# Moving the second sample's soma products and gelu, and one GpSimd addition, in the start of a four-layer conditioned residual kernel

## The chip, the core and the metric

The kernel runs on one core of a Trainium2 chip. A core has a matrix engine (TensorE, PE in the profile; its weight loads are PEld), a vector engine (VectorE, DVE), an activation engine (ScalarE, ACT), GpSimd (POOL) and a queue that issues transfers (SyncE, SP). Each works off its own queue in order and waits on semaphores for the others. The metric is the device time of one execution in microseconds, the median of several runs.

## What is computed

The input x has 16 samples of 256 positions and 256 channels. Four layers follow one another, each added to its input:

```python
# layer 0, per sample: 16 causal traces
ctx      = causal_ema(x, tau_ctx)                      # h = alpha*h + b_t along the positions
gated    = x * sigmoid([x, ctx] @ Wg.T + bg)
mod      = 0.5 + sigmoid(gelu(x @ Wn1.T + bn1) @ Wn2.T + bn2)         # one row per trace
temporal = sum_d causal_ema(gated * mod[..., d], tau[d]) * softmax(blend)[d]
gate     = sigmoid(temporal @ Wtemp.T + btemp)
soma     = gelu(x @ Wsoma.T + bsoma)
x        = x + layernorm((soma * gate) @ Wout.T) * gamma + beta
# layer 1: pooling over the positions
scores   = tanh(x @ W1 + b1) @ v
x        = x + (softmax(masked scores) @ x) / count
# layer 2: 8 experts and a shared one, gated per sample
x        = x + sum_e coef[e] * ((silu(x @ Wg[e]) * (x @ Wu[e])) @ Wd[e])
# layer 3: gelu(x @ W1 + b1) @ [W2, We[index]] + bias, added to x
```

## The kernel before

**Precision.** A float32 operand is split into a rounded high part and the difference to it. A product is then three products on TensorE: high by high, high by low, low by high (`mm3`, L105 to L107). High parts are made by ScalarE's copy (`rnd`, L92), low parts by a subtraction on VectorE or GpSimd (`low`, L99). The small weights (gate, soma, temp, out and others) lie in `small_a` and `small_b` and are split into `wh` and `wl` by `high_small` (L141) and `low_small` (L99).

**Stages.** `traces(b)` is layer 0 of sample b up to the temporal sum, `pooled(b)` is the rest of layer 0 and layer 1. Layers 2 and 3 take the samples in pairs and stream expert weights in chunks (`w_e`) of 128 rows: `load_chunk` transfers a raw chunk (L792) into one of four raw places, ScalarE rounds it (L92), VectorE or GpSimd makes its low part (L99), and ten such chunks make a ring. A unit of layer 2 (`l2_unit`) makes `pg` and `pu` for two chunks, ScalarE's silu (L865), VectorE's product (L866), a split of the hidden layer (`hh`), and two units later the product back down (`y`). `pg` and `pu` share three PSUM buffers.

**The start.** Sample 0 goes first and alone through `first_traces` and `first_pooled`, which multiply unsplit float32. In `first_traces` ScalarE scales the modulation (L625), GpSimd multiplies it with the gated input (L628, traces 1 to 15), VectorE scans (L631) and TensorE sums the traces (L635). At its end GpSimd adds beta to sample 0's input `xt` (L655); the layer norm adds the result (L695). `first_pooled` is a chain: `pt` (L668), tanh, `po` (L682), statistics of the layer norm, a power on GpSimd (L690), L695, transposes `ptr` (L703), `pa` (L710), tanh (L714), the scores `psc` (L717), masked maximum (L725) and exp (L728), normalisation (L736), transposes `ppt` (L741), `pp` (L749), the sum `acc` (L753) and its split, with which layer 2 starts.

**Between these steps** stand those of the second sample, `second_traces` (L334): its context scan, `ph` and a gelu (L350), the gate products in two halves (`gates_of`, L363 to L365), the modulation, the soma products in two halves of six (`soma_half`), and two gelus into `sm` (L402). Then `blended` does its 16 traces: VectorE's products `bt` (L417) and scans (L421), GpSimd's running sum `ta` (L425), with modulation rows that SP loads in pairs (`mod`, L412).

**What sets the order.** `ORDER0` says by hand which of the two generators steps next (p: `first_pooled`, t: `second_traces`; each `yield` ends a step). `extra` puts other work behind numbered steps, `tc.issue_after(i)` puts instructions behind another in order of issue, and the framework's scheduler settles the rest for each engine. After the start, steps of the following samples are spread over the units of layer 2 by a pace (`pace`, `due`). Sample 0 goes alone through the first five experts; then sample 1 joins.

Of the kernel before, what the change touches and what calls it, by code (L numbers as in the profile page):

```python
# [8 lines left out]
F32 = mybir.dt.float32  # L9
F32R = mybir.dt.float32r  # L10
I32 = mybir.dt.int32
AF = mybir.ActivationFunctionType
ALU = mybir.AluOpType
# [4 lines left out]
S = 256  # L18
P = 128
# [3 lines left out]
RING = 10  # L23
FRONT = 4

ORDER0 = "pptptptptptptptptpt"
FRONT0 = ORDER0.count("t")
SECOND_STEPS = FRONT0 + 17
SLACK = 16
# [13 lines left out]
O_N1, O_G, O_SO, O_TE, O_OU, O_W1, W_COLS = 0, 256, 1280, 1792, 2304, 2816, 3072  # L43

V_BG, V_BN1, V_BN2, V_BSO, V_BTE, V_B1, V_V, V_L3B1, V_B2, V_WN2, V_COLS = 0, 2, 3, 4, 6, 8, 9, 10, 18, 19, 67
# [3 lines left out]
def fused_kernel(  # L49
# [21 lines left out]
    V, G, A, PE = nc.vector, nc.gpsimd, nc.scalar, nc.tensor  # L71
# [12 lines left out]
    ps_y = ctx.enter_context(tc.tile_pool(name="ps_y", bufs=1, space=PSUM))  # L84
# [3 lines left out]
    last_of = {}  # L88
# [9 lines left out]
    def low(e, out_, in_, h):  # L98
        i = (V if e == "v" else G).tensor_tensor(out_, in_, h.bitcast(F32), ALU.subtract)  # L99
        if e == "v":  # L100
            last_of["cv"] = i
        return i

    def mm3(o, wh, wl, xh, xl, start, stop, **kw):
        PE.matmul(o, wh, xh, start=start, stop=False, **kw)  # L105
        PE.matmul(o, wh, xl, start=False, stop=False, **kw)  # L106
        last_of["pe"] = PE.matmul(o, wl, xh, start=False, stop=stop, **kw)  # L107
# [7 lines left out]
    def load_xt(b):  # L115
        xt = xin.tile([P, 2, S], F32, tag="xt", name=f"xt{b}", bufs=1)
        nc.sync.dma_start(xt, x[b])
        return xt

    def const(shape, dtype, name, src, q=nc.scalar):  # L120
        t = cp.tile(shape, dtype, name=name)
        q.dma_start(t, src)
        return t
# [7 lines left out]
    def small(off, n):  # L131
        if O_TE <= off < O_W1:
            return raw_b[:, off - O_TE : off - O_TE + n]
        c = off if off < O_TE else off - O_W1 + O_TE
        return raw_a[:, c : c + n]
# [7 lines left out]
    def low_small(c0, n, e):  # L143
        low(e, wl[:, c0 : c0 + n], small(c0, n), wh[:, c0 : c0 + n])
# [6 lines left out]
    vec = const([P, V_COLS], F32, "vec", vecs)  # L151
# [7 lines left out]
    xt_tiles = {0: load_xt(0)}  # L159
    gam = const([P, S], F32, "gam", gamma.partition_broadcast(P), nc.sync)  # L160
    bet = const([P, S], F32, "bet", beta.partition_broadcast(P), nc.sync)
# [81 lines left out]
    def W(part, off, n):  # L243
        t = wh if part == 0 else wl
        return t[:, off : off + n]
# [13 lines left out]
    def ft(tag, name, bufs=1):  # L259
        return l0.tile([P, 2, S], F32, tag=tag, name=name, bufs=bufs)  # L260
# [68 lines left out]
    def soma_half(pso, xh, xl, m):  # L329
        for k in range(2):  # L330
            o = O_SO + k * S + m * P
            mm3(pso[:, m], W(0, o, P), W(1, o, P), xh[:, k], xl[:, k], k == 0, k == 1)

    def second_traces():  # L334


        xh, xl = early_x.pop(1)
        xr = xin_tiles.pop(1)
        cx = ft("ta", "ctx1")
        for c in range(2):  # L340
            V.tensor_tensor_scan(
                cx[:, c], decay[:, ND : ND + 1].to_broadcast([P, S]), xr[:, c], 0.0, ALU.mult, ALU.add
            )
        yield
        ph = ps_y.tile([P, 512], F32, tag="y1", name="ph1")
        for k in range(2):
            o = O_N1 + k * P
            mm3(ph[:, :S], W(0, o, P), W(1, o, P), xh[:, k], xl[:, k], k == 0, k == 1)
        hg = l0.tile([P, S], F32, tag="hg", name="hg1")
        last_of["ca"] = A.activation(hg, ph[:, :S], AF.Gelu, bias=vec[:, V_BN1 : V_BN1 + 1])  # L350
        ch, cl = hl("c_1", "hA")
        rnd("a", ch, cx)
        hs = l0.tile([P, S], F32R, tag="hs", name="hs1")
        rnd("a", hs, hg)
        pg = ps_y.tile([P, 2, S], F32, tag="y0", name="pg1")

        def gates_of(ks):
            for m in range(2):
                for k in ks:
                    o = O_G + k * S + m * P  # L360
                    i, j = (xh[:, k], xl[:, k]) if k < 2 else (ch[:, k - 2], cl[:, k - 2])
                    kw = dict(skip_group_check=True)
                    PE.matmul(pg[:, m], W(0, o, P), i, start=k == 0 and m == 0, stop=False, **kw)  # L363
                    PE.matmul(pg[:, m], W(0, o, P), j, start=False, stop=False, **kw)
                    last_of["pe"] = PE.matmul(pg[:, m], W(1, o, P), i, start=False, stop=k == 3, **kw)  # L365

        with tc.issue_after(last_of["chain"].ins):
            gates_of((0, 1))
        yield
        low("v", cl, cx, ch)  # L370
        yield
        low("v", hs[64:], hg[64:], hs[64:])
        yield
        pm = ps_gu.tile([P, 512], F32, tag="gu", name="pm1")
        with tc.issue_after(last_of["chain"].ins):
            PE.matmul(pm[:48, :S], n2[:, 0], hs, start=True, stop=False)
            last_of["pe"] = PE.matmul(pm[:48, :S], n2[:, 1], hs, start=False, stop=True)
        yield
        with tc.issue_after(last_of["chain"].ins):
            gates_of((2, 3))  # L380
        pso = ps_y.tile([P, 2, S], F32, tag="y1", name="pso1")
        with tc.issue_after(last_of["pe"].ins):
            soma_half(pso, xh, xl, 0)
        md = l0.tile([48, S], F32, tag="md", name="md1")
        A.activation(md, pm[:48, :S], AF.Tanh, bias=hb[:48, V_BN2 : V_BN2 + 1], scale=0.5)
        ga = ps_a.tile([P, 2, S], F32, tag="ga", name="gp1")
        for m in range(2):
            last_of["ca"] = A.activation(
                ga[:, m], pg[:, m], AF.Tanh, bias=hb[:, V_BG + m : V_BG + m + 1], scale=0.5
            )  # L390
        yield
        V.tensor_scalar(md, md, 0.5, 1.0, ALU.mult, ALU.add)
        mdd = dram.tile([1, ND, S], F32, tag="mdd", name="mdd1")
        nc.sync.dma_start(mdd[0], md[0:ND])
        yield
        last_of["cv"] = V.scalar_tensor_tensor(ga, ga, 1.0, xr, ALU.add, ALU.mult)
        yield
        with tc.issue_after(last_of["chain"].ins):
            soma_half(pso, xh, xl, 1)
        sm = ft("sm", "sm1")  # L400
        for m in range(2):
            last_of["ca"] = A.activation(sm[:, m], pso[:, m], AF.Gelu, bias=vec[:, V_BSO + m : V_BSO + m + 1])  # L402
        yield
        yield from blended(1, ga, mdd, sm, None)

# [159 lines left out]
    def first_traces():  # L565
# [27 lines left out]
        ms = l0.tile([48, S], F32R, tag="ths", name="ms0")  # L593
        rnd("v", ms, md)
        low("v", ms[32:], md[32:], ms[32:])

        with tc.issue_after(last_of["md"].ins):
            for off in (O_G, O_G + 512):
                high_small(off, 512)
        for off in (O_G, O_G + 512):  # L600
            low_small(off, 512, "g")
        yield
        ga = ft("ga", "ga0")
        with tc.issue_after(last_of["pm"].ins):
# [8 lines left out]
        sm = ps_a.tile([P, 2, S], F32, tag="ga", name="sm0")  # L613

        tacc = [ps_y.tile([P, 512], F32, tag=f"y{c}", name=f"ta0{c}")[:, :S] for c in range(2)]
        for d in range(ND):
# [19 lines left out]
            if d == 5:  # L636
                pso = ps_l.tile([P, 2, S], F32, tag="ps", name="pso0")
# [5 lines left out]
            if d in (9, 11):  # L643
                m = (d - 9) // 2
# [5 lines left out]
        for c in range(2):  # L650
            evict(c, t[:, c], tacc[c])
        last_of["t"] = last_of["ca"]
        xt = xt_tiles.pop(0)
        with tc.issue_after(last_of["g"].ins):
            last_of["g"] = G.tensor_tensor(xt, xt, bet.unsqueeze(1).to_broadcast([P, 2, S]), ALU.add)  # L655
        held[0] = xt, sm, t
        yield

# [340 lines left out]
    def prefetch(n, boost=BOOST, later=None):  # L999
        while n > 0 and nxt[0] < len(order):  # L1000
            k = order[nxt[0]]
            if k[0] == "c" and k[1] not in eregs:
                eregs[k[1]] = nc.sync.value_load(eix[0:1, k[1] : k[1] + 1], min_val=0, max_val=NE - 1)
            with tc.high_priority(offset=boost) if boost else nullcontext():
                load_chunk(k, later)
            nxt[0] += 1
            n -= 1
# [24 lines left out]
    def feed():  # L1032
        gens, left = {}, {}
        for i, phase in enumerate(phases):
# [14 lines left out]
            live = set(phase)  # L1049
            fixed = list(ORDER0) if i == 1 else []  # L1050
            while live:
# [38 lines left out]
        high_small(O_SO, 512)  # L1090
        low_small(O_SO, 512, "g")

    low_later = []

    def high_parts():
        prefetch(2, 0, low_later)
        for off, n in ((O_TE, 512), (O_OU, 512), (O_W1, 256)):
            high_small(off, n)

    def low_parts(*small_ones):  # L1100
        while low_later:
            low(*low_later.pop(0))
        for off, n in small_ones:
            low_small(off, n, "v")

# [1 line left out]
        5: high_parts,  # L1107
        9: low_parts,
        15: lambda: low_parts((O_TE, 512)),
        17: lambda: low_parts((O_OU, 512), (O_W1, 256)),  # L1110
    }
    with tc.issue_after(last_of["t"].ins):
        weights_on_gpsimd()
    for i in range(1, len(ORDER0) + 1):
        beside(lambda: next(steps))
        if i in extra:
            beside(extra[i])
    n = 4
    with tc.issue_after(last_of["ca"].ins), tc.issue_after(last_of["cv"].ins):
        coefs()  # L1120
        prefetch(RING - n)
# [155 lines left out]
```

## Time and profile before

| What | us |
|---|---|
| three runs | 2819.82, 2822.01, 2822.59 (median 2822.01) |
| the profiled execution | 2821.16 |
| its span, from the first to the last instruction | 2819.1 |
| TensorE busy / VectorE / ScalarE / GpSimd | 2769.4 / 1455.0 / 1242.8 / 1301.6 |
| mean granted TensorE clock | 0.996 of full |
| TensorE busy, 300 to 2819 | 2505.6 of 2519.0 |
| TensorE busy, 160 to 180 | 10.4 of 20, granted clock 0.74 |
| VectorE busy, 70 to 120 | 50.0 of 50 |
| GpSimd busy, 70 to 120 | 46.5 of 50 |

A row of a timeline is: start, duration, engine, line, operation, output and inputs, shapes, and in brackets the idle time of the engine before it with what ended it. In order of time the start looks so: first traces to 35.3, layer norm about 42, scores about 48, layer 2 from 55.5, silu from 62.2. From 164 to 174 TensorE is mostly idle; it then has no more work of sample 0 alone, and `pooled(1)` is not through yet. Full-clock products of 128x256 follow one another every 0.12 us there, and every 0.21 us at half clock. The names `gp` and `sm` are the second sample's gate and soma, `pso` the PSUM of its soma products.

### The profile page before, as it was taken

What the parts mean: (1) busy time and instruction counts of PE and PEld (TensorE: products, weight loads), DVE (VectorE), ACT (ScalarE), POOL (GpSimd) and SP (SyncE); (2) the same over time, 40 slices, a digit from 0 to 9 for tenths busy, and PEclk for the clock granted to TensorE, in tenths of its full rate; (3) what the DMA queues carried; (4) which work ended last, traced back from release to release, by engine and by line L of the source; (5) the groups of instructions that cost most, each with busy time, mean ns of one, the idle gap of its engine ahead of it and who ended that gap; (6) DMA issues with size and microseconds to landing.
All of it is one profiled execution on the core that took longest, in us unless ns stands there. A gap on an engine that the chain in (4) does not pass through costs nothing.

```text
span 2819.1 us, 37035 instructions
## 1 busy us (share of the span) xinstructions
PE 2769.4 (98%) x13636; PEld 2337.7 (83%) x13636; DVE 1455.0 (52%) x2664; ACT 1242.8 (44%) x2060; POOL 1301.6 (46%) x984
## 2 busy tenths in 40 slices
PE   8889999999999999999999999999999999999999
PEld 6878798888888888888888888888888888888888
DVE  7989876766665453544545445454444542222222
ACT  6555564565444433435334443334433453333334
POOL 5946545644554453544534444443444443333333
PEclk9999999999999999999999999999999999999999
DMA  5543376395443533324433143331523252222453
GB/s 144 164 137 107 103 251 215 117 321 189 152 158 106 174 109 109 116 81 152 142 113 99 48 174 110 116 119 53 177 101 113 92 170 91 90 90 90 168 177 118
DMA packets 116998, 377.53 MB, mean 134 GB/s; under 512 B 12898, under 2 KB 31186, under 8 KB 116818
## 3 DMA queue, kind: packets, MB, share of 16 engines
q1 hardware_dynamic: 116386, 375.11, 40.5%
q8 instruction: 108, 1.77, 0.3%
q14 instruction: 72, 0.59, 0.1%
q10 hardware_dynamic: 432, 0.06, 0.0%
HBM read 310.91 MB, written 64.21 MB: 133 GB/s over the span
## 4 chain that ended last, share of the span: by engine, by line
PE 88%; DVE 6%; ACT 2%; issue 2%; DMA 2%; SPq 0%; DVEq 0%; POOL 0%; ACTq 0%
PE pg L105 9%; PE pg L106 9%; PE pg L107 9%; PE pu L105 8%; PE pu L107 8%; PE pu L106 8%; PE y L107 8%; PE y L105 8%; PE y L106 8%; DVE w_e L99 1%; DVE tr L421 1%; PE z L105 1%; PE z L106 1%; PE z L107 1%; DMA raw_e<-in_wexp_dram 1%
## 5 line engine op out<-in xcount | busy, mean ns | idle before, releaser
L99 POOL TENSOR_TENSOR hh<-h,hh 128x512 fp32r<-128x512 f32 x640 | 848.2, 1326 | 1314.2 <-ACT hh L92 1294.8
L866 DVE TENSOR_TENSOR h<-h,pu 128x512 f32<-128x512 f32 x576 | 393.7, 683 | 904.4 <-PE pu L107 809.0
L92 ACT ACTIVATE hh<-h 128x512 fp32r<-128x512 f32 x640 | 403.6, 631 | 954.8 <-DVE h L866 932.1
L105 PE MATMUL pg<-x,w_e 128*128 128x512 f32 (+1 forms) x1232 | 465.8, 378 | 8.9 <-DVE h L866 8.9
L865 ACT ACTIVATE h<-pg 128x512 f32<-128x512 f32 x576 | 342.5, 595 | 298.0 <-PE pg L107 235.1
L105 PE MATMUL pu<-x,w_e 128*128 128x512 f32 (+1 forms) x1232 | 464.7, 377 | 7.0 <-ACT h L865 6.0
L106 PE MATMUL pg<-x,w_e 128*128 128x512 f32 (+1 forms) x1232 | 463.9, 377 | 0.0
L107 PE MATMUL pg<-x,w_e 128*128 128x512 f32 (+1 forms) x1232 | 463.6, 376 | 0.0
L106 PE MATMUL pu<-x,w_e 128*128 128x512 f32 (+1 forms) x1232 | 463.5, 376 | 0.0
L107 PE MATMUL pu<-x,w_e 128*128 128x512 f32 (+1 forms) x1232 | 463.4, 376 | 0.0
L106 PE MATMUL y<-hh,w_e 128*128 128x512 f32 (+1 forms) x1232 | 462.6, 376 | 0.6 <-POOL hh L99 0.6
L107 PE MATMUL y<-hh,w_e 128*128 128x512 f32 (+1 forms) x1232 | 462.4, 376 | 0.0
L105 PE MATMUL y<-hh,w_e 128*128 128x512 f32 (+1 forms) x1232 | 415.6, 376 | 0.0
L425 POOL TENSOR_TENSOR ta<-ta,tr 128x512 f32<-128x512 f32 x225 | 311.1, 1382 | 66.2 <-DVE tr L421 55.2
L421 DVE TENSOR_TENSOR_SCAN tr<-decay,bt 128x256 f32<-128x256 f32 x450 | 284.6, 671 | 0.0
L105 PEld LDWEIGHTS pg<-x,w_e 128*128 128x128 f32 x1232 | 232.3, 189 | 51.8 <-DVE h L866 11.8
L105 PEld LDWEIGHTS pu<-x,w_e 128*128 128x128 f32 x1232 | 232.6, 189 | 49.7 <-ACT h L865 7.8
L106 PEld LDWEIGHTS y<-hh,w_e 128*128 128x128 f32 x1232 | 231.9, 188 | 43.3 <-POOL hh L99 1.8
L107 PEld LDWEIGHTS pu<-x,w_e 128*128 128x128 f32 x1232 | 232.5, 189 | 41.9
L107 PEld LDWEIGHTS pg<-x,w_e 128*128 128x128 f32 x1232 | 232.0, 188 | 41.8
L107 PEld LDWEIGHTS y<-hh,w_e 128*128 128x128 f32 x1232 | 231.8, 188 | 41.9
L106 PEld LDWEIGHTS pu<-x,w_e 128*128 128x128 f32 x1232 | 232.4, 189 | 40.8
(308 smaller groups left out, 3275.0 us busy)
## 6 DMA issues: line engine op xcount, KB each, us to landing
w_e<-keep_e SPq DMA_DIRECT2D x216, 768.0 KB, 4.3
keep_e<-w_e SPq DMA_DIRECT2D x72, 768.0 KB, 4.3
raw_e<-in_wexp_dram SPq DMA_DIRECT2D x112, 384.0 KB, 4.5
mod<-mdd SPq DMA_DIRECT2D x120, 256.0 KB, 3.8
w_f<-keep_f SPq DMA_DIRECT2D x56, 384.0 KB, 3.5
spare<-in_wexp_dram SPq DMA_DIRECT2D x48, 384.0 KB, 3.2
raw_c<-in_comb_dram SPq DMA_DIRECT2D x32, 260.0 KB, 2.9
xr<-in_xT_dram SPq DMA_DIRECT2D x16, 256.0 KB, 3.3
```

The source lines that it names most:

```text
L92: last_of["ca"] = A.activation(out_, in_, AF.Copy)
L99: i = (V if e == "v" else G).tensor_tensor(out_, in_, h.bitcast(F32), ALU.subtract)
L105: PE.matmul(o, wh, xh, start=start, stop=False, **kw)
L106: PE.matmul(o, wh, xl, start=False, stop=False, **kw)
L107: last_of["pe"] = PE.matmul(o, wl, xh, start=False, stop=stop, **kw)
L421: V.tensor_tensor_scan(tr[:, c], decay[:, d : d + 1].to_broadcast([P, S]), bt[:, c], 0.0, ALU.mult, ALU.add)
L425: G.tensor_tensor(tacc, tacc, tr, ALU.add)
L865: A.activation(h, ps_g, AF.Silu)
L866: last_of["h"] = V.tensor_tensor(h, h, ps_u, ALU.mult)
```

## The change

Four edits, all in the first 65 us of the program.

1. **Soma products.** All twelve products of the second sample's soma are issued behind the first half of its gate products, ahead of the transposes `ptr`. Before, six stood behind the second half of the gate products, ahead of `ppt`, and six behind `pp`.
2. **Gelu.** The two gelus into `sm` stand ahead of the scores: behind the eviction of `ptr`, ahead of tanh at L714. In the built program ScalarE has one table load fewer. `second_traces` has one step fewer, and `ORDER0` one t fewer.
3. **Beta.** GpSimd's addition of beta to sample 0's `xt` moves from the end of `first_traces` to its second step. The two weight differences of the gate (`low_small`, GpSimd) are issued behind it.
4. **Chunk 4.** One chunk more is loaded in the start: its rounding on ScalarE stands ahead of the split of sample 0's `x`, its low part on VectorE behind that split.

Each engine runs as many products, traces and differences as before. The scheduler also orders many instructions between about 60 and 155 us differently: on VectorE products `bt` stand further ahead of scans, on GpSimd some `hh` and `w_e` differences change places with running sums, and on SP some `mod` loads stand ahead of chunk loads. Behind that the order is the same.

```diff
-ORDER0 = "pptptptptptptptptpt"
+ORDER0 = "pptptptptptptptptp"
...
         with tc.issue_after(last_of["chain"].ins):
             gates_of((0, 1))
+        pso = ps_y.tile([P, 2, S], F32, tag="y1", name="pso1")
+        with tc.issue_after(last_of["pe"].ins):
+            for m in range(2):
+                soma_half(pso, xh, xl, m)
         yield
         low("v", cl, cx, ch)
         yield
         low("v", hs[64:], hg[64:], hs[64:])
+        sm = ft("sm", "sm1")
+        for m in range(2):
+            last_of["ca"] = A.activation(sm[:, m], pso[:, m], AF.Gelu, bias=vec[:, V_BSO + m : V_BSO + m + 1])
         yield
...
         with tc.issue_after(last_of["chain"].ins):
             gates_of((2, 3))
-        pso = ps_y.tile([P, 2, S], F32, tag="y1", name="pso1")
-        with tc.issue_after(last_of["pe"].ins):
-            soma_half(pso, xh, xl, 0)
...
         last_of["cv"] = V.scalar_tensor_tensor(ga, ga, 1.0, xr, ALU.add, ALU.mult)
-        yield
-        with tc.issue_after(last_of["chain"].ins):
-            soma_half(pso, xh, xl, 1)
-        sm = ft("sm", "sm1")
-        for m in range(2):
-            last_of["ca"] = A.activation(sm[:, m], pso[:, m], AF.Gelu, bias=vec[:, V_BSO + m : V_BSO + m + 1])
         yield
...
         low("v", ms[32:], md[32:], ms[32:])
+        xt = xt_tiles.pop(0)
+        last_of["xt"] = G.tensor_tensor(xt, xt, bet.unsqueeze(1).to_broadcast([P, 2, S]), ALU.add)
...
-        for off in (O_G, O_G + 512):
-            low_small(off, 512, "g")
+        with tc.issue_after(last_of["xt"].ins):
+            for off in (O_G, O_G + 512):
+                low_small(off, 512, "g")
...
-        xt = xt_tiles.pop(0)
-        with tc.issue_after(last_of["g"].ins):
-            last_of["g"] = G.tensor_tensor(xt, xt, bet.unsqueeze(1).to_broadcast([P, 2, S]), ALU.add)
         held[0] = xt, sm, t
...
-    low_later = []
+    low_later, low_last = [], []
...
-    def low_parts(*small_ones):
-        while low_later:
-            low(*low_later.pop(0))
+    def low_parts(*small_ones, of=low_later):
+        while of:
+            low(*of.pop(0))
...
         15: lambda: low_parts((O_TE, 512)),
+        16: lambda: prefetch(1, 0, low_last),
         17: lambda: low_parts((O_OU, 512), (O_W1, 256)),
+        18: lambda: low_parts(of=low_last),
...
-    n = 4
+    n = 5
     with tc.issue_after(last_of["ca"].ins), tc.issue_after(last_of["cv"].ins):
         coefs()
         prefetch(RING - n)
```

## The prediction

> **What bounds the kernel now.** I read the page's busy rows first, then windows of TensorE as long as a step of its granted clock, then the timeline of each engine over the first 65 us, then the chain from there to 200.
>
> ```profile
> span 2819.1 us, 37035 instructions
> PE 2769.4 (98%) x13636; PEld 2337.7 (83%) x13636; DVE 1455.0 (52%) x2664; ACT 1242.8 (44%) x2060; POOL 1301.6 (46%) x984
> ```
>
> TensorE is the bound, and the change adds and removes none of its products. A change can act only on the 50 us in which TensorE idles and on the time it runs at half clock. Both lie mostly before 200: after 300 TensorE is busy 2505.6 of 2519.0. All edits lie before 65, and from about chunk 42 the order of every queue is the old one. So the question is what moves before 200.
>
> The window view (columns: window, length, PE busy and count, granted clock, DMA share, GB/s):
>
> ```profile
> 41.17:44.58 3.41, 1.56 (x12) 1.00 0.54 156
> 44.58:47.99 3.41, 3.27 (x8) 0.50 0.56 129
> 48.00:51.41 3.41, 3.41 (x15) 0.50 0.77 244
> 51.41:54.82 3.41, 2.99 (x19) 1.00 0.26 88
> 58.24:61.65 3.41, 1.89 (x16) 1.00 0.24 62
> ```
>
> The layer norm leaves TensorE busy for 1.56 of 3.41 us, and the next two windows run at half clock; a window with 1.89 did not lose it.
>
> The timeline of GpSimd, the tile view of beta, and the timeline of ScalarE:
>
> ```profile
> 11.78 2.68 POOL L99 TENSOR_TENSOR wl<-small_a,wh 128x512 fp32r<-128x512 f32 x2 [10.39 <-ACT wh L141]
> 15.56 18.44 POOL L628 TENSOR_TENSOR bt<-ga,mod 128x512 f32<-128x512 f32 x15 [1.11 <-ACT mod L625]
> 33.97 1.26 POOL L655 TENSOR_TENSOR xt<-xt,bet 128x512 f32<-128x512 f32 x1
> ```
>
> ```profile
> L122 SPq DMA_DIRECT2D bet<-in_beta_dram x1: 430/430/430, 7.7 to 7.7; - x1
> DMA to landing us min/median/max: 6.4/6.4/6.4
> ```
>
> ```profile
> 54.99 0.85 ACT L92 ACTIVATE x<-acc 128x256 fp32r<-128x256 f32 x2 [2.11 <-DVE acc L753]
> 55.86 1.28 ACT L402 ACT_TABLE_LOAD   x1
> 57.16 0.84 ACT L402 ACTIVATE sm<-pso,vec 128x256 f32<-128x256 f32 x2
> 57.88 0.84 ACT L92 ACTIVATE w_e<-raw_e 128x768 fp32r<-128x768 f32 x1
> 58.62 1.57 ACT L92 ACTIVATE w_e<-spare 128x768 fp32r<-128x768 f32 x2
> 60.09 0.84 ACT L92 ACTIVATE w_e<-raw_e 128x768 fp32r<-128x768 f32 x1
> 60.94 1.28 ACT L865 ACT_TABLE_LOAD   x1
> 62.24 1.09 ACT L865 ACTIVATE h<-pg 128x512 f32<-128x512 f32 x2
> ```
>
> GpSimd makes the fifteen trace products without a gap, and the last scan ends at 35.31, one pair (1.3) after the last product: GpSimd paces the first traces. In the last fence ScalarE goes from the split of the first sample to the first silu through a table load, a gelu, four chunk casts and a second load, while TensorE, with its three PSUM buffers full, waits 2.76 (its next product is at 62.89).
>
> **Part 1: beta.** GpSimd's addition now stands first in its queue and waits for beta. That landed at 7.75 + 6.4 = 14.15; the transfers ahead of it are unchanged. The addition ends at 14.15 + 1.26 = 15.4, the two weight differences queued behind it (2.68) at 18.1, and the first product on GpSimd starts there and not at 15.56: **+2.5**. Ends: 0 if beta landed before 10, +3.0 if the addition is stretched (1.74 is the longest at L433). I take 2.5, since it is the same transfer. ScalarE's scalings, the scans and TensorE's sums wait for these products, so the whole first chain moves. The 1.26 given back at 33.97 buys nothing on the chain: the power at L690 follows 0.1 behind the weight difference of the soma products, but waits for VectorE's L689, which is late by 2.5 too. That difference ends at 41.96 + 2.5 - 1.26 = 43.2, and the moved soma products first need it about 44.5.
>
> **Part 2: soma products in the gap.** Before, the gate products end issue at 41.78 and the transposes start at 43.43: a gap of 1.65. Twelve products at the pitch of 0.12 fill 1.44; cost nothing, with 0.2 to spare. What they may bring is the clock: 1.56 + 1.44 = 3.0 in that window, above the 1.89 that held full clock. At full clock pa (L710, four in 2.06) costs what two pairs at L668 do, 0.43 + 0.59 = 1.0, and psc (L717, 1.22) about 0.65. tanh and the exp table load come 1.0 earlier, the maxima 1.6; the first exp (48.88) waits for both, the load would end at 47.4: **-1.4**. The Trainium skill speaks against this (TensorE: Matmul & The Clock Gate, "HAM oscillation"): only idle gaps over about 3.4 us cost the clock. By it a gap of 1.65 did no harm, and filling it is worth 0; by the windows it is worth 1.4. The granted clock did fall here, so I take 1.4, with 0 as the other end.
>
> The six products removed at 51.03 stood between the normalised scores (ready 50.92) and their transposes (51.91): **-0.95**. The six at 54.58 ran while x was split (54.99): 0.
>
> First unit's products: 2.5 - 1.4 - 0.95 = +0.15, so 55.6 for 55.48.
>
> **Part 3: ScalarE.** The load and the gelu go: 57.88 - 55.86 = 2.02. The gelu, still within gelu's and tanh's table (no load stands between L350 and L714), goes behind the eviction ending 44.48 and ahead of tanh at 46.63; with the shorter pa 1.1 us remain for 0.84. If that cover were gone it would cost up to 0.84. Chunk 4's cast (pitch 0.74) moves into the idle 2.11 ahead of 54.99, its transfer issued at 38.95. ScalarE is thus ahead by 2.76 - 0.15 = **2.6**: silu at 59.6, just as TensorE fills its third buffer. The Trainium skill (ScalarE: Activation LUTs, "What ACT_TABLE_LOAD costs") prices a switch at 2.66, a drain of 1.38 included; by it this part gains 4.0. But here the load starts 0.02 behind x and the gelu 0.02 behind the load, so I take 1.28.
>
> VectorE's waits of 1.83, 1.24 and 0.66 before its first h (62.87) shrink alike: h at 60.2. From 62.87 to 121.4 VectorE has no idle gap in its timeline, so it carries these 2.6 us through the second sample's traces.
>
> **Part 4: order.** The scheduler reshuffles the queues from 60 to 155. On GpSimd one hidden-layer difference (1.3) comes ahead of the last running sum, on VectorE one h (0.66) ahead of t; VectorE starts t 2.0 after that sum, so only the 0.66 counts: **+0.6**. On SP the mod loads of traces 10, 12 and 14 step ahead of chunk loads 19, 20 and 23; each waits for a VectorE product that now comes earlier, and a late one holds the chunk behind it (3.3 to landing). Ends 0 and +3.3; I take 0. At 164 to 193 TensorE waits for the second sample, so its arrival sets the end: -2.6 + 0.6 = **-2.0**.
>
> The profiled execution took 2821.16 (span 2819.1), 0.85 below the median of 2822.01. So 2819.2 for it, and **2820.0** for the median.
>
> **Rivals.**
>
> *More comes than was moved (0.25).* The chain has soft places downstream. VectorE idles 0.98 and 1.47 between 121 and 125 for casts that waited on chunks, and TensorE runs 18 products from 173.9 at 0.21 and not 0.12 because the wait for the second sample cost its clock (1.7). Without them: -2.6 - 2.45 - 1.7 = -6.8, 2815.2. For it: fewer waits early give chunks a lead. Against: the same four raw buffers limit that lead.
>
> *A chunk wait gets ahead of the traces (0.23), slower.* ScalarE, VectorE and SP are queues in order. In the new order VectorE does two chunk differences (10, 11) between the fourth products and the third scans. A turn is transfer, cast and difference:
>
> ```profile
> 98.68 3.28 DMA raw_e<-in_wexp_dram
> 118.81 3.60 DMA spare<-in_wexp_dram
> 163.53 3.13 DMA spare<-in_wexp_dram
> ```
>
> Three such transfers are on the chain already. Each more costs 3.3 + 0.85 + 0.96 = 5.1; with two of them: -2.0 + 10.2 = +8.2, 2830.2. It decides from the second on. For it: VectorE has no slack there. Against: the transfers the new order needs first are issued some 2.6 earlier too.
>
> *The clock falls all the same (0.07).* Then 1.4 is lost and silu is ahead by about 1.2: -0.6, 2821.4. That the soma products do nothing for time is this case.
>
> **How the numbers follow.** The main case has 0.45, from -4.5 (order free, +0.6 gone, a half-clock window of 3.41 us less, 1.7) to +1 (beta's 3.0, gelu's 0.84, one window more); 0.05 of it spills past -5.6. A measurement of this kernel tells about 0.2% (5.6 us) from no change. Faster: 0.25 + 0.05 = 0.30; slower: 0.22 of the third case; same: 0.48. The range takes in the more-case down to 2813.5 and half of the slower case, to 2829.0; the main case alone is 2817.5 to 2823.
>
> **What would show it.** GpSimd's first trace product at 18.1, the layer norm's transposes near 45.9 with twelve soma products ahead; full clock in every window from 41 to 55; ppt near 52; no table load between ppt and the first silu; that silu near 59.6 and TensorE's wait before it below 0.5; VectorE without gaps from 60 on; the second sample's t at 124.5. If beta lands earlier, part 1 falls and the gain grows by up to 2.5; if the first trace product is late but VectorE shows new gaps on chunk casts between 65 and 120, the slower case is there.

## The result and the profile after

| | before | after |
|---|---|---|
| median of 11 runs | 2820.88 us | 2827.27 us |
| range | 2818.89 to 2825.07 | 2825.16 to 2831.49 |
| the profiled execution | 2821.16 | 2826.54 |

The ratio is 1.0023, with a 95% interval of 1.0015 to 1.0032: slower by 6.4 us, where 2820.0, 2.0 below the median known then, and no visible difference were forecast.

The first two lines of the page of the changed kernel:

```profile
span 2824.8 us, 37031 instructions
...
PE 2775.0 (98%) x13636; PEld 2343.3 (83%) x13636; DVE 1461.8 (52%) x2664; ACT 1240.5 (44%) x2059; POOL 1301.1 (46%) x984
```

VectorE does as many instructions as before in 6.8 us more: some of them take longer. Where the 5.7 us of span arise is seen by following the same instructions in both traces (starts in us; the last column is after less before):

| milestone | before | after | |
|---|---|---|---|
| first trace product on GpSimd | 15.56 | 18.49 | +2.9 |
| sample 0's t on ScalarE | 35.52 | 41.27 | +5.8 |
| split of sample 0's x | 54.99 | 58.02 | +3.0 |
| first silu | 62.24 | 62.33 | +0.1 |
| first h on VectorE | 62.87 | 64.81 | +1.9 |
| sample 1's t on ScalarE | 124.64 | 132.45 | +7.8 |
| split of sample 1's x | 184.12 | 190.47 | +6.3 |
| silu at 2745 | 2744.99 | 2750.63 | +5.6 |

Nearly everything is decided before 190; from there to the end the silus are 5.3 to 6.4 late. There are two losses, at 15 to 41 and at 60 to 130, and between them gains of the size that was forecast.

**The first loss.** The timeline of GpSimd, that of TensorE, and the window view in steps of 3.41 us (window, length, PE busy and count, then the other engines, granted clock, DMA share, GB/s), all of the changed kernel:

```profile
14.35 1.27 POOL L595 TENSOR_TENSOR xt<-xt,bet 128x512 f32<-128x512 f32 x1 [12.96 <-DMA bet<-in_beta_dram]
15.58 2.94 POOL L99 TENSOR_TENSOR wl<-small_a,wh 128x512 fp32r<-128x512 f32 x2
18.49 11.08 POOL L629 TENSOR_TENSOR bt<-ga,mod 128x512 f32<-128x512 f32 x9
```

```profile
20.52 1.80 PE L636 MATMUL ta<-tr,ident 128*128 128x256 f32 x4 [2.12 <-DVE tr L632]
22.25 0.79 PE L621 MATMUL pb<-ms,sel 48*128 48x256 f32 x2
22.97 3.78 PE L636 MATMUL ta<-tr,ident 128*128 128x256 f32 x8
```

```profile
17.20:20.61 3.41, 1.29 (x7) 0.77 (x5) 1.11 (x3) 0.84 (x2) 3.41 (x4) 1.00 0.99 390
20.61:24.02 3.41, 3.41 (x9) 2.07 (x10) 3.41 (x6) 2.24 (x7) 3.41 (x4) 0.53 0.14 51
...
30.85:34.26 3.41, 3.41 (x15) 2.36 (x15) 2.75 (x6) 1.06 (x3) 2.56 (x3) 0.97 0.00 0
```

GpSimd waits for beta and the traces start 2.9 late, as forecast within 0.4. But TensorE, which sums the traces, has too little to do meanwhile: it is busy for 1.29 of 3.41 us. The clock falls for 10.2 us, eight sums take 3.78 and not 1.99, VectorE's scans then wait for TensorE, and +2.9 becomes +5.8.

**The gains.** The layer norm's windows and ScalarE's timeline, changed kernel:

```profile
41.09:44.50 3.41, 3.41 (x18) 2.80 (x18) 1.10 (x3) 2.60 (x6) 3.41 (x3) 1.00 0.20 23
44.50:47.92 3.42, 3.42 (x24) 3.21 (x24) 3.30 (x10) 3.39 (x7) 1.78 (x3) 1.00 0.62 207
```

```profile
58.02 0.80 ACT L92 ACTIVATE x<-acc 128x256 fp32r<-128x256 f32 x2 [1.43 <-DVE acc L751]
...
61.04 1.28 ACT L863 ACT_TABLE_LOAD   x1
62.33 0.60 ACT L863 ACTIVATE h<-pg 128x512 f32<-128x512 f32 x1
```

The layer norm keeps full clock, and from t to the split of x 2.7 us are won against the profile of before (forecast 2.35). This is not shown to be the work of the moved soma products. Three of the kernels below (e2, e8, e16) leave the soma products where they were, and each has its window over the layer norm at another place than the profile of before. The window view of TensorE alone, of e8, e2 and e16 in this order:

```profile
40.01:43.42 3.41, 1.91 (x16) 1.00 0.57 202
43.42:46.84 3.42, 2.21 (x17) 1.00 0.39 121
39.16:42.58 3.42, 2.29 (x17) 1.00 0.66 229
```

They keep full clock there, and from t to the split of x they take 17.05, 16.74 and 17.03 us; the changed kernel takes 16.75, and only the profile of before takes 19.47. So the moved products win nothing where the clock holds; how often the kernel before loses it there is open.

One table load stands between the split and the silu: another 2.9 (2.76).

**The second loss.** VectorE's timeline before (first fence) and in the changed kernel, and the one line of GpSimd's beside the latter:

```profile
56.22 0.18 DVE L239 COPY coef<-sgt 128x16 f32<-128x16 f32 x1
56.43 0.17 DVE L240 TENSOR_SCALAR sgt<-sgt 128x16 f32<-128x16 f32 x1
```

```profile
59.19 0.95 DVE L99 TENSOR_TENSOR w_e<-raw_e,w_e 128x768 fp32r<-128x768 f32 x1
60.06 1.84 DVE L239 COPY coef<-sgt 128x16 f32<-128x16 f32 x1
61.93 1.76 DVE L240 TENSOR_SCALAR sgt<-sgt 128x16 f32<-128x16 f32 x1
63.73 0.29 DVE L241 TENSOR_TENSOR coef<-gat,sgt 128x128 f32<-128x128 f32 x1
63.94 0.95 DVE L99 TENSOR_TENSOR w_e<-raw_e,w_e 128x768 fp32r<-128x768 f32 x1
64.81 0.68 DVE L864 TENSOR_TENSOR h<-h,pu 128x512 f32<-128x512 f32 x1
```

```profile
59.63 4.03 POOL L99 TENSOR_TENSOR w_e<-spare,w_e 128x768 fp32r<-128x768 f32 x2 [6.08 <-ACT w_e L92]
```

Before, the copy and the scaling of the coefficients (16 columns) took 0.18 and 0.17. Chunk 4's low part (59.19) now stands ahead of them, so they come beside GpSimd's pair of differences. GpSimd's first difference ends at 61.86 and the copy at 61.90; the second ends at 63.66 and the scaling at 63.69: each waits for GpSimd's running instruction, 3.3 us in all, of which 1.9 reach h (the silu it needs ends at 62.9).

The pair of differences has moved too: it starts 1.6 behind the split of x and not 4.5, since ScalarE's casts come earlier there. This alone is enough. In e5, which has the moved gelu and no chunk 4, the pair starts 2.35 behind the split, and the next two instructions wait for it:

```profile
55.69 0.17 DVE L239 COPY coef<-sgt 128x16 f32<-128x16 f32 x1
...
56.96 1.94 DVE L241 TENSOR_TENSOR coef<-gat,sgt 128x128 f32<-128x128 f32 x1
58.83 2.58 DVE L99 TENSOR_TENSOR w_e<-raw_e,w_e 128x768 fp32r<-128x768 f32 x1
```

h comes 6.8 behind the split of x in e5 and e7, without chunk 4, as in the changed kernel with it.

From the first h to 134 it is VectorE's chunk differences that grow. The groups by form, before (56 to 130) and in the changed kernel (56 to 134):

```profile
L99 DVE TENSOR_TENSOR w_e<-raw_e,w_e 128x768 fp32r<-128x768 f32 x10 | 13.6, 1364 | 4.5 <-ACT w_e L92 4.5
L99 DVE TENSOR_TENSOR w_e<-spare,w_e 128x768 fp32r<-128x768 f32 x8 | 10.2, 1274 | 1.0 <-ACT w_e L92 1.0
...
L99 DVE TENSOR_TENSOR w_e<-raw_e,w_e 128x768 fp32r<-128x768 f32 x10 | 15.9, 1590 | 2.2 <-ACT w_e L92 2.2
L99 DVE TENSOR_TENSOR w_e<-spare,w_e 128x768 fp32r<-128x768 f32 x8 | 13.4, 1670 | 0.0
```

Eighteen differences take 29.3 us against 23.8, while scans, products and h are equal to 0.1: the differences fall beside other GpSimd instructions than before.

### The profile page after: what moved, and what is told of

Read it like the earlier page. It is cut to its first block, busy times and chain, and to the rows that moved or that the text cites. A ratio compares the mean times of both kernels' runs of the same rounds, so it can differ in the third digit from the quotient of the medians.

```text
span 2824.8 us, 37031 instructions
## 1 busy us (share of the span) xinstructions
PE 2775.0 (98%) x13636; PEld 2343.3 (83%) x13636; DVE 1461.8 (52%) x2664; ACT 1240.5 (44%) x2059; POOL 1301.1 (46%) x984
## 4 chain that ended last, share of the span: by engine, by line
PE 88%; DVE 6%; ACT 2%; issue 2%; DMA 2%; POOL 0%; SPq 0%; DVEq 0%; ACTq 0%
PE pg L105 9%; PE pg L106 9%; PE pg L107 9%; PE pu L105 8%; PE pu L107 8%; PE pu L106 8%; PE y L107 8%; PE y L105 8%; PE y L106 8%; DVE w_e L99 1%; DVE tr L419 1%; DMA raw_e<-in_wexp_dram 1%; PE z L105 1%; PE z L107 1%; PE z L106 1%
## 5 line engine op out<-in xcount | busy, mean ns | idle before, releaser
L105 PEld LDWEIGHTS pu<-x,w_e 128*128 128x128 f32 x1232 | 232.9, 189 | 46.3 <-ACT h L863 4.3
L106 PEld LDWEIGHTS y<-hh,w_e 128*128 128x128 f32 x1232 | 232.4, 189 | 43.3 <-POOL hh L99 1.8
L107 PEld LDWEIGHTS y<-hh,w_e 128*128 128x128 f32 x1232 | 232.4, 189 | 41.9
L107 PEld LDWEIGHTS pu<-x,w_e 128*128 128x128 f32 x1232 | 232.5, 189 | 41.8
L105 PEld LDWEIGHTS y<-hh,w_e 128*128 128x128 f32 x1232 | 231.8, 189 | 42.3 <-ACT hh L92 0.4
```

## The experiments

Theory: (A) beta ahead of the weight differences makes the traces late, and the fall of TensorE's clock doubles that; (B) chunk 4's low part moves VectorE's coefficients and differences beside GpSimd's differences. Rival 1: beta is the whole loss. Rival 2: only the new order on VectorE is.

A profile of these kernels is read with care: of the thirteen profiles without prewarmed start, full clock is first granted at 8.9 to 10.8 in seven and at 14.5 to 15.6 in six. The kernel before, e1, e5, e6 and e9 run the same instructions for the first 40 us, and three of them (e1, e5, e6) got it late; their first trace product comes at 17.5 to 17.8, that of the other two at 14.8 and 15.6. So verdicts come from medians of 11 runs, against the kernel before on the same chip. A difference has an interval of about 2.5 us to either side, so two variants that are less than 2 to 3 us apart are not told apart:

| kernel | median | before | difference | ratio, 95% interval |
|---|---|---|---|---|
| changed | 2827.27 | 2820.88 | +6.4 | 1.0023 [1.0015, 1.0032] |
| e1 beta back | 2823.86 | 2821.05 | +2.8 | 1.0007 [0.9998, 1.0016] |
| e2 beta only | 2825.59 | 2821.05 | +4.5 | 1.0016 [1.0007, 1.0025] |
| e3 beta behind | 2823.93 | 2821.05 | +2.9 | 1.0008 [0.9999, 1.0017] |
| e4 coefficients early | 2824.45 | 2821.05 | +3.4 | 1.0013 [1.0004, 1.0022] |
| e5 soma and gelu only | 2819.41 | 2820.50 | -1.1 | 0.9989 [0.9979, 0.9998] |
| e6 = e1 + e4 | 2821.46 | 2820.50 | +1.0 | 1.0003 [0.9994, 1.0012] |
| e7 no chunk 4 | 2821.30 | 2820.50 | +0.8 | 1.0002 [0.9993, 1.0011] |
| e8 chunk 4 only | 2826.33 | 2820.50 | +5.8 | 1.0017 [1.0008, 1.0027] |
| e9 = e5, coefficients early | 2817.26 | 2821.26 | -4.0 | 0.9986 [0.9977, 0.9995] |
| e11 changed, fill | 2826.90 | 2821.26 | +5.6 | 1.0017 [1.0008, 1.0026] |
| e12 = e9, beta behind | 2817.59 | 2821.26 | -3.7 | 0.9988 [0.9979, 0.9997] |
| e13 = e9, prewarmed | 2818.54 | 2821.55 | -3.0 | 0.9991 [0.9982, 1.0000] |
| e14 = e11, prewarmed | 2823.05 | 2821.55 | +1.5 | 1.0009 [1.0000, 1.0018] |
| e15 changed, prewarmed | 2825.88 | 2821.55 | +4.3 | 1.0017 [1.0008, 1.0027] |
| e16 before, prewarmed | 2820.71 | 2821.55 | -0.8 | 0.9998 [0.9989, 1.0007] |

**e1, e2, e3: beta.** e1 puts the addition back, e2 moves it alone, e3 lets the differences go first:

```diff
         low("v", ms[32:], md[32:], ms[32:])
-        xt = xt_tiles.pop(0)
-        last_of["xt"] = G.tensor_tensor(xt, xt, bet.unsqueeze(1).to_broadcast([P, 2, S]), ALU.add)
...
+        for off in (O_G, O_G + 512):
+            o = wh[:, off : off + 512]
+            last_of["wl"] = low("g", wl[:, off : off + 512], small(off, 512), o)
+        xt = xt_tiles.pop(0)
+        with tc.issue_after(last_of["wl"].ins):
+            last_of["xt"] = G.tensor_tensor(xt, xt, bet.unsqueeze(1).to_broadcast([P, 2, S]), ALU.add)
```

> The changed kernel with one edit undone: GpSimd's addition of beta stands at the end of the first traces again, and the two weight differences do not wait for it. Theory (late traces through beta and TensorE's clock, and besides VectorE's coefficients and weight differences stretched by GpSimd in the new order): GpSimd's first trace product is back at 15.6, no half-clock window at 20 to 31, sample 0's last t at 35.5, the first split of x about 52 and the first silu about 59.4; the stretched VectorE part stays, so the second sample arrives only some 3 to 4 us earlier than in the changed kernel: about 2823. Rival 1 (beta is the whole loss): all 6.3 us of the arrival come back and the gains of the soma products and the gelu show as well: 2817 or less. Rival 2 (only the new order on VectorE counts, the early loss being absorbed): 2827, as the changed kernel.

> The kernel before with the beta edit alone. Theory: the first trace product at 18.5, TensorE loses its clock at about 20.6 and sample 0's t is 5.7 late; with nothing to win it back the first silu and the second sample are late by about as much: 2825 to 2826.5. Rival 1 (beta is the whole loss) gives at least the changed kernel's loss, 2827 or more, since the gains of the soma products and the gelu are missing. Rival 2 (only the new order counts): within 1 us of the kernel before.

> The changed kernel with GpSimd's beta addition behind the two weight differences and ahead of the trace products. The differences need no beta, so they end near 14.5 and the addition fills what would be idle. Theory: the first trace product starts at 15.7 to 15.9 and not at 18.5, TensorE keeps its clock, t near 35.6, and the time is that of the kernel with beta back at its place, about 2823 (a little less if the 1.26 us freed at 34 matter). Rival 1 (beta is the whole loss): 2817. If the loss sat in the addition itself and not in the place it waits at, it would stay at 2826 to 2827.

Without the wait for beta the changed kernel is 3.6 us faster, and in e3 the same addition costs nothing: its place costs, not its work. Half of the loss stays, as the theory said (2823), and not 2817: rival 1 falls. e2 costs 4.5, of which 1.7 arise elsewhere: in its trace, and in those of e8, e13 and e16, VectorE, GpSimd and ScalarE do some steps at 190 to 215 in another order, and each of the four loses 1.7 there (e2's delay goes from 2.25 to 3.93). So beta alone is about 2.8, and rival 2 falls too.

In e1 and e3 the first product comes at 17.57 and 18.03, not at 15.6, because their profiled executions got full clock late (14.6 and 15.5). In such an execution beta's place costs next to nothing, since the first product is late anyway: sample 0's t stands at 38.03 in e4, with beta ahead, and at 37.78 in e6, with beta at the end, both with late full clock. With early full clock it stands at 41.27 in the changed kernel and at 35.52 before. The 3.6 us between medians are presumably a mixture of both.

**e4, e6: the coefficients.**

```diff
-        15: lambda: low_parts((O_TE, 512)),
+        15: lambda: (low_parts((O_TE, 512)), coefs()),
...
-        coefs()
         prefetch(RING - n)
```

> The changed kernel with the coefficients of layer 2 (three small VectorE instructions) issued ahead of chunk 4's low part instead of behind it. Beta stays as in the changed kernel. Theory: the copy and the scaling take 0.2 us each again and not 1.8, the first product on VectorE comes 2 to 3 us earlier (about 62.5), and the second sample arrives about that much earlier unless VectorE's weight differences, still stretched beside GpSimd's, keep it: 2824 to 2825. Rival 1 (beta is the whole loss): no change, 2827.

> The changed kernel with two things put right: beta's addition at its old place and the coefficients ahead of chunk 4's low part. Measured so far against the kernel before: changed kernel +6.4, beta back +2.8, coefficients early +3.4 us. Theory: the two are different stalls and add, 6.4 - 3.6 - 3.0 = -0.2: about 2821, the same as the kernel before; what is then missing against the gain of the soma products and the gelu (2 to 4 us) lies in VectorE's weight differences beside GpSimd's. Rival 1 (beta is the whole loss): no better than beta back alone, 2823.9.

VectorE's timeline in e4:

```profile
52.47 0.17 DVE L239 COPY coef<-sgt 128x16 f32<-128x16 f32 x1
...
59.83 0.69 DVE L864 TENSOR_TENSOR h<-h,pu 128x512 f32<-128x512 f32 x1 [0.29 <-ACT h L863]
```

The copy takes 0.17 again. h comes 4.9 behind the split of x (54.93) and not 6.8 as in the changed kernel, and of the median 3.0 us come back. Both repairs give 5.4 together, near the sum of 6.6. (The profiled execution of e4, 2820.85, is the fastest of its eleven.)

**e5, e7, e8, e9, e12: which parts are worth having.** e5 leaves only soma products and gelu, e7 leaves out chunk 4, e8 has it alone in the kernel before; e9 is e5, and e12 e5 with e3's beta, both with e4's edit. Chunk 4 goes by

```diff
-        16: lambda: prefetch(1, 0, low_last),
...
-        18: lambda: low_parts(of=low_last),
...
-    n = 5
+    n = 4
```

> The changed kernel without the beta edit and without the chunk 4 edit: only the soma products and the gelu are moved. Theory (beta costs about 4 through the late traces, chunk 4 costs 3 or more because VectorE's coefficients and differences fall beside GpSimd's): the coefficients take 0.2 us each again, the first product on VectorE comes about 2.6 earlier than in the kernel before for the same start, and the time is 2 to 4 us under the kernel before: about 2818. Rival 1 (beta is the whole loss): the same as with beta alone put back, 2823.9. Rival 2 (the moved products and gelu win nothing that reaches the end): 2821.

> The changed kernel without the chunk 4 edit; beta stays ahead of the traces. Theory: chunk 4 is what pushes the coefficients beside GpSimd's differences and what reorders VectorE's queue, so this is better than the changed kernel by 3 to 5 us: 2822 to 2824, and worse than the kernel with only the soma products and the gelu by beta's 4. Rival 1 (beta is the whole loss): as the changed kernel, 2827.

> The kernel before with the chunk 4 edit alone: its rounding ahead of the split of x, its low part behind that split and ahead of the coefficients, and the queue order that the scheduler makes of it. Theory: ScalarE's cast falls in the idle 2 us ahead of the split, the coefficients are stretched only if GpSimd's pair of differences has begun (it begins at 59.5 in the kernel before, some 3 us behind the coefficients), so they stay short here and what is seen is the new order of VectorE's differences beside GpSimd's: 0 to 4 us slower, 2821 to 2825. Rival 1 (beta is the whole loss): within 1 us of the kernel before.

> Only the soma products and the gelu are moved, as in the kernel of that name (2819.41), and besides the coefficients are issued ahead of the split of x. There the coefficient product took 1.94 us and the weight difference behind it 2.58, both beside GpSimd's pair of differences. Theory (VectorE waits for GpSimd's running instruction): the product is back at 0.3 us, the weight difference starts 1.6 earlier but still waits for GpSimd, so the first product on VectorE comes 0.5 to 1.6 us earlier: 2818 to 2819. Rival (the stretched instructions have their cover, ScalarE's silu being the later of the two): 2819.4.

> Everything of the change but chunk 4, with both stalls taken out: soma products and gelu moved, coefficients early, and beta's addition behind the two weight differences and not ahead of them. Theory: beta now costs at most 0.2 (it fills GpSimd's wait for the first scaling) and frees 1.26 us of GpSimd at 34, where nothing waits for it; the time is that of the kernel with the soma products, the gelu and early coefficients: 2818 to 2819. If beta's place at the end of the first traces was itself a cost, it is better than that one by up to 1 us.

Chunk 4 costs the changed kernel 5.6 us (e7). The coefficients are not part of it: e6 and e9 both have them early and beta at its old place and differ by chunk 4 alone, and chunk 4 costs 5.0 us there too. What it brings is its order of VectorE's queue. From the first h to sample 1's t a chunk difference on VectorE takes 1.55 to 1.79 us on the mean in the nine profiles with chunk 4, and 1.29 to 1.44 in the eight without it; from that h to the split of sample 1's x it is 123.9 to 127.2 us with chunk 4 and 121.3 to 124.0 without. Which exchange in the order does it, no run shows.

e7 is only 1.9 above e5, where beta was expected to cost 4; this is not told apart from the 3.6 of e1. e5 gains less than expected, 1.1. Its eleven runs fall into two groups, five at 2815.4 to 2816.0 and six at 2819.4 to 2821.6, and the median is the lowest of the upper group, to which the profiled execution belongs; what separates them no trace shows. With the coefficients out of the way (e9) all runs lie at 2815.3 to 2819.0: the moved products and gelu gain 4.0 together with the early coefficients, more than expected, and e9 is faster than both kernels. What the coefficients add to e5 is not clear of the noise. e12 equals e9: beta in the right place costs nothing and brings nothing.

e8 was expected at up to +4, took +5.8, and has two causes besides the longer differences: the order at 190 to 215 (1.7) and a wait for a chunk. VectorE's timeline in e8, where sample 1 had been 6.0 us early at its t:

```profile
167.29 0.15 DVE L521 TENSOR_TENSOR sums<-sums,cntb 128x2 f32<-128x2 f32 x1
170.50 0.96 DVE L99 TENSOR_TENSOR w_e<-raw_e,w_e 128x768 fp32r<-128x768 f32 x1 [3.06 <-ACT w_e L92]
171.38 0.16 DVE L522 RECIPROCAL sums<-sums 128x2 f32<-128x2 f32 x1
```

A chunk difference stands inside sample 1's normalisation and waits for its cast, and the cast waits 3.16 us for its transfer. This is the prediction's slower rival, but in e8's order, not in that of the changed kernel: there VectorE waits for no cast from 65 to 130.

**e10: GpSimd beside VectorE by itself.** Nothing of the layers is computed.

> The disputed cost by itself; nothing of the layers is computed and the outputs are zeros. VectorE does, eight times in turn, a copy and a scaling of 128x16, a difference of 128x768 from two SBUF operands, a three-operand product of 128x256, a scan of 128x256 and a product of 128x512 with one operand in PSUM, first beside 96 sums of 128x512 on GpSimd in a row, then alone. Theory: copy, scaling and difference end only when GpSimd's running sum has ended (up to 1.3 us more, 0.6 on the mean, and GpSimd's next sum then waits for them); three-operand product, scan and PSUM product take the same time in both passes (0.47, 0.68, 0.66). Rival (a shared bandwidth): all six are longer by the same share in the first pass.

The groups of instructions by form (span 162.5 us):

```profile
L106 DVE TENSOR_TENSOR_SCAN sn<-sc,b 128x256 f32<-128x256 f32 x16 | 27.9, 1744 | 0.0
L104 DVE SCALAR_TENSOR_TENSOR st<-a,sc,b 128x256 f32<-128x256 f32 x16 | 23.6, 1477 | 0.0
...
L108 DVE TENSOR_TENSOR hh<-a,pz 128x512 f32<-128x512 f32 x16 | 10.5, 655 | 0.0
L98 DVE COPY o<-a 128x16 f32<-128x16 f32 x16 | 9.1, 569 | 0.0
```

Both passes ran beside GpSimd's sums, so there is no pass alone. The product with one operand in PSUM keeps its 0.66 with 1.1 us of a sum still to go. The copy waits: it starts 0.56 before a sum's end and takes 0.59. Not all forms are longer by the same share, so the rival "shared bandwidth" falls.

Against the expectation, three-operand product and scan wait as well (1.48, 1.74), while in the changed kernel the products `bt` and the scans `tr` take 0.47 and 0.67 beside GpSimd as elsewhere, over a hundred times each. The code has the difference: the bench takes all operands from SBUF, but in the kernel `bt` reads `gp` (pool `ps_a`) and `tr` reads the decays (pool `ps_l`), and both lie in PSUM. With one operand in PSUM none was held up (`bt`, `tr`, h and the bench's PSUM product); with both in SBUF three-operand product and scan were. The bench's difference met no running sum; in the kernel it is one that waits, and both its operands lie in SBUF.

**e11, e14, e15, e16, e13: TensorE's clock.** e11 repeats the first soma product of sample 0 while TensorE waits; the others put products of the identity at the very start:

```diff
+                    for _ in range(4):
+                        PE.matmul(pso[:, 0], small(O_SO, P), xr[:, 0], start=True, stop=True)
...
         ph = ps_l.tile([P, 512], F32, tag="ps", name="ph0")
+        for _ in range(9):
+            PE.matmul(ph[:, :P], ident, ident, start=True, stop=True)
```

> The changed kernel with the first of sample 0's soma products done four times more on TensorE (2 us of work whose result is overwritten), where it waits for the late trace products at 18.4 to 20.5. Theory: no half-clock windows at 20 to 31; the first trace product stays at 18.5, but the last t is 2.9 late and not 5.7, and the time is under the changed kernel's by up to 2.8 us, as far as its executions lose the clock there: 2825 to 2826. Rival (the clock there is no matter, the late products are all of beta's cost): 2827, or later by the added work.

> The kernel before with nine products of the identity with itself on TensorE from 1.5 us on, whose result is overwritten: TensorE is busy while it would wait for the first weights, so that full clock is granted in every execution before the gate products. The profiles so far show full clock from 9 to 11 in seven kernels and from 14.5 to 15.6 in six. Theory (the start's clock is a matter of when TensorE's first busy window ends): full clock from 5 to 9, the first trace product at 15.5 or a little earlier in each execution, executions closer together, and the median 0.5 to 2 us lower: 2819 to 2820.5. Rival (the spread has another cause): the same median and the same range.

> The changed kernel with the same nine products ahead. Beta still lands at 14, so GpSimd's first trace product stays at about 18.3. Theory: with full clock early in each execution TensorE has less to do and idles longer for the late trace products, so the clock falls at 20 to 31 in each execution and not in some: no gain from the prewarmed start, 2827 to 2830, 8 or more above the kernel before with the same products. Rival 1 (the clock at 20 to 31 is no matter): 2825.5, the gain of the start and beta's 2.9.

> The changed kernel with the nine products ahead and the four repeated soma products in TensorE's wait for the late trace products. Theory: full clock early and kept at 20 to 31 in each execution; 2 to 3 us below the changed kernel with the nine products alone: 2825 to 2826.5; what remains above the kernel before is beta's 2.9 and chunk 4's part. Rival 1 (the clock there is no matter): the same as without the fill.

> Soma products and gelu moved, coefficients early, no beta and no chunk 4 edit, and the nine products ahead. Without them it took 2817.26 beside 2821.26 of the kernel before. Theory: the prewarmed start adds to it, since it saves the 2 us of a late full clock where that occurs and some half-clock gate products otherwise: 2815 to 2816.5. Rival: 2817.3.

e11 is only 0.8 better than the changed kernel, each against the kernel before; its profiled execution got full clock at 15.6, where nothing is lost at 20 to 31 even without the fill (e4, from 14.95 on). With prewarmed starts full clock comes at 4.6 to 6.2 in all four profiles, but little follows for the median. e15 took 2825.88, not 2827 or more; e16 gains 0.8, which is not distinguishable from zero; e13 does not add to e9. e13 and e16 have the other order at 190 to 215, which takes back 1.7. e14 is better than expected by 2 us.

TensorE's timeline in e15:

```profile
15.26 1.13 PE L638 MATMUL ta<-tr,ident 128*128 128x256 f32 x4
19.80 2.08 PE L638 MATMUL ta<-tr,ident 128*128 128x256 f32 x4 [3.42 <-DVE tr L634]
```

It idles 3.42 and runs at half clock from 18.7 to 25.5; in e14, with the fill, it keeps full clock to 83, and t comes at 37.15 and not at 38.42. VectorE, ScalarE and GpSimd have the same order in both. Of these 1.3 us, 0.6 are there already at the first trace product (17.18 and 17.77), and at the split of sample 1's x e14 is 1.9 later than e15, so the traces do not carry the gain to the end. Between the medians e14 is 2.8 faster, and the intervals overlap. That the clock falls and what it costs at t is shown: in the changed kernel's own trace the rise from 2.9 to 5.8. What it costs at the end is open.

## Why the prediction failed, step by step

- **Part 1, beta (+2.5): too small, the step that failed first.** The queue was right, the first product came 2.9 late. But "so the whole first chain moves" took the delay to pass on unchanged. The same window rule that earned part 2 its 1.4 (1.56 of 3.41 us busy lost the clock) had to be applied to TensorE's wait that part 1 itself makes: 1.29 busy, and t came 5.8 late. Between medians beta costs 3.6 (e1). The Trainium skill (TensorE: Matmul & The Clock Gate, "HAM oscillation") would have let it pass too, with its gap of about 3.4 us: the longest gap here was 2.12.
- **Part 2, soma products (-1.4 - 0.95): the number came by luck.** 2.7 was measured between the two profiles. But the lost clock belonged to the one profile of before that was read, not to its order: e2, e8 and e16 have the old order, keep the clock, and are as fast from t to the split of x as the changed kernel. The 0.95 is not there either when the clock holds.
- **Part 3, ScalarE (-2.6): right as far as ScalarE goes (2.9), wrong in what follows.** "It carries these 2.6 us through the second sample's traces" failed. ScalarE's earlier casts also start GpSimd's differences earlier, and VectorE's coefficients, or what follows them, wait for these: +3.3 on VectorE, and h at 64.8, not at 60.2. VectorE had no idle gap, as forecast, but its instructions are no fixed sizes. The Trainium skill (SBUF — State Buffer, "Who interferes with whom") says that a copy, a scaling, or an operation with both inputs in SBUF can share a port with GpSimd and is then blocked for GpSimd's whole instruction; the copy's 1.84 and the scaling's 1.76, ending 0.03 to 0.04 behind GpSimd's, agree. It exempts an instruction with at most one input in SBUF, outside the modes that use two ports; `bt` and `tr`, 0.47 and 0.67 beside GpSimd, agree too.
- **Part 4, order (+0.6): too small, by the medians the step that cost most.** The order was taken as single instructions stepping ahead; what it did was choose who stands beside whom. Chunk 4's cast was priced by itself; the order that comes with its low part costs, with it, 5.6 us (e7), and 5.0 with the coefficients early (e6 less e9). VectorE's differences take 5.4 more by 134.
- **Rivals.** The slower rival had the right side and a price near (2830.2) by the wrong mechanism, which is luck; its wait did occur in e8. The case in which the clock falls was put at the layer norm, where it held.

The 6.4 us add up when one part after another is taken out of the changed kernel: 5.6 for chunk 4 (e7), 1.9 for beta (e7 less e5), and -1.1 for soma products and gelu (e5). In the other order beta is 3.6 (e1) and chunk 4 is 3.9 (e1 less e5). Each of these has the interval given above.

## What to carry to other kernels

When work is put into an engine's wait, ask what it itself waits for and what is queued behind it: behind the two weight differences beta's addition was free, ahead of them it cost 3.6 us. When a delay passes an engine whose clock depends on being busy, price its idle window as well. And before instructions on VectorE are moved, or GpSimd's are made earlier, look which will stand beside which: three coefficients out of the way were worth 3 us, and chunk 4, in whose order the differences are longer, cost 5. A window that loses the clock in one profile need not lose it in the next: compare several before a gain is built on it.

## What was not expected of the hardware

- A copy of 16 columns on VectorE takes 0.17 us alone and 1.84 beside a difference on GpSimd; it ends 0.04 behind it. Three-operand product and scan take 1.48 and 1.74 us beside GpSimd's sums with all operands in SBUF (e10), and 0.47 and 0.67 beside GpSimd with one operand in PSUM (the changed kernel).
- Kernels with the same first 40 us get full clock first at 8.9 and 10.5 or at 14.5 to 15.2, which moves the first traces by 2 us; nine products at 1.45 us bring it to 4.6 to 6.2 (median of the kernel before: -0.8, not distinguishable from zero).
- Two edits that touch only the first 35 us (e2, e16) changed the built order at 190 to 215, for 1.7 us.
